# Selective scans on one core: three of eight B diagonals loaded from DRAM, softplus terms added by DMAs, the rate product made once

## The chip, the core and the metric

The kernel runs on one core of a Trainium2 chip. The metric is device time in microseconds (us) for one launch. The core has a matrix engine (PE, with its weight loads shown as PEld), a vector engine (DVE), an activation engine (ACT), a general engine (POOL), an engine that mainly issues transfers (SP), and 16 DMA engines. Each engine works through its own instructions in program order and waits on semaphores for the others.

## What is computed

Two layers run one after the other on an image of 256 x 256 tokens with 128 channels, all in float32. The first is a row-wise attention with four heads. The second, which takes most of the time, is a selective state-space layer. Its core, cut to what matters here:

```python
delta = jax.nn.softplus(dts + dt_bias[None, :, :, None])
def step(h, inp):
    d_t, x_t, B_t, C_t = inp
    dA = jnp.exp(d_t[..., None] * As)
    h = dA * h + (d_t * x_t)[..., None] * B_t[:, :, None, :]
    y = jnp.einsum('bkdn,bkn->bkd', h, C_t)
    return (h, y)
```

It runs over 65,536 tokens in four orders (along the rows, across them, and both backwards), with 256 inner channels and 16 states per channel. `dts` is itself a product of an 8-row matrix with a small weight (the "rate product").

## The kernel before

`scans` does the four orders one after the other. A `Block` is 1,024 tokens of one order; there are 64 blocks per order, 256 in all. Channels lie on partitions, in two halves of 128 (`h`), and tokens lie along the free dimension. For each block the body runs 32 steps `s`; step `s` is state `m = s // 2` and half `h = s % 2`. One step has these parts, on these engines:

- **recur** (L853): the recurrence itself is one DVE scan instruction over 1,024 tokens (L858). It reads the decay `da` (SBUF) and the input `mm` (PSUM) and writes `hs`. After the second half a small DVE reduction saves the state (L863), and POOL multiplies both halves of `hs` by C, held in `cc` (L865).
- **turn** (L841): PE writes delta * x * B, turned so that channels lie on partitions, into `mm`. There are only two `mm` buffers, used in rotation, so turn of step s+1 goes into one while the scan of step s reads the other. The 1,024 tokens are eight tiles of 128. For four of them (`DJ`) PE multiplies `dxt` by a diagonal matrix `dg` whose diagonal holds B (L846); a float32 product takes two instructions. For the other four ACT has already scaled `dxt` by B into `but`, and PE only transposes that (L848, one instruction).
- **scale** (L830): ACT makes the diagonals, `dg = identity * B` (L833), and the scaled tiles `but` (L835), three states ahead of use. Rings `dg`, `but` and `cc` have four places.
- **decay** (L837): ACT makes `da = exp(delta * A)` (L839), four steps ahead.
- **collect** (L869): PE transposes the `hs` tiles, after POOL's multiply, and adds them up in the PSUM tiles `y` (L617), three states behind. `share` sets how many a step takes.
- **fetch** (L825): SP issues the load of one row of C to all partitions, 512 KB, into `cc[m % 4]`; it waits until POOL has finished with that place.

Between those, each block prepares its successor: `begin` returns a list of pieces, each with the step at which it is issued, before or after that step's scan. `rate` (steps 6 and 8, L750) writes the rate product into an `mm` buffer, ACT takes its absolute value (L759), then exp, log, one plus and one minus (L762 to L774, 2,048 elements each). POOL adds two correction terms to the log at steps 11 to 14 (L780, L777). At steps 18 and 20 `rate` makes the same product again, and DVE forms `delta = max(product, 0) + lw` (L783). At steps 22 and 24 PE turns `delta` (`turn_rate`, L790, again in an `mm` buffer) and DVE multiplies it by x (`times_x`, L794). At steps 6 and 8 DVE adds the finished `y` to the running output (`evict`, L898). All loads of the stage are issued by SP: at step 0 `load_tokens` loads B (`bt`, 64 KB, L727) and x (`xk`, 1 MB, L728) for the next block, at step 8 the output is stored (L902), at step 16 it is loaded (L948), at step 21 come the rates (L724). The order is written out by hand in `body` (L908).

Of the kernel before, what the change touches and what calls it, by code (L numbers as in the profile page):

```python
# [29 lines left out]
AF = mybir.ActivationFunctionType  # L30
ALU = mybir.AluOpType
# [588 lines left out]
def scans(tc, io, c):  # L620
# [19 lines left out]
    with tc.tile_pool(name="e_w", bufs=1) as wp, tc.tile_pool(name="e_1", bufs=1) as sb1, tc.tile_pool(  # L640
# [11 lines left out]
        def ring(name, n, shape, pool=wp):  # L652
            return [pool.tile(shape, F32, name=f"{name}{i}") for i in range(n)]

        DJ = NJ // 2
        xks = ring("xk", 1, [P, NJ, DI])

        dts = ring("dt", 1, [P, TB])
# [26 lines left out]
        class Block:  # L685
# [39 lines left out]

            def load_tokens(self):
                nc.sync.dma_start(out=self.as_rows(self.bt), in_=self.rows(io["bk"][self.S.k]))  # L727
                nc.sync.dma_start(out=self.as_rows(self.xk), in_=self.rows(io["xk"]))  # L728

            def advance(self, now, after):  # L730
                if self.pieces is None:
# [5 lines left out]
        def begin(B):  # L737
# [19 lines left out]

            def size(h):
                nc.scalar.activation(B.e[:, h, :], B.pu[h], AF.Abs)  # L759

            def exp():
                nc.scalar.activation(B.e, B.e, AF.Exp, scale=-1.0)  # L762
# [10 lines left out]

                nc.scalar.activation(B.w, B.w, AF.Identity, scale=-1.0, bias=1.0)  # L774

            def less(h):
                nc.gpsimd.tensor_tensor(B.lw[:, h, :], B.lw[:, h, :], B.w[:, h, :], ALU.add)  # L777

            def log1p(h):
                nc.gpsimd.tensor_tensor(B.lw[:, h, :], B.lw[:, h, :], B.e[:, h, :], ALU.add)  # L780

            def softplus(h):
                nc.vector.scalar_tensor_tensor(B.delta[:, h, :], B.pu[h], 0.0, B.lw[:, h, :], ALU.max, ALU.add)  # L783

            def turn_rate(i):
                B.pt = mm().rearrange("p (j d) -> p j d", d=DI)
# [5 lines left out]
            def times_x(i):  # L792
# [12 lines left out]
                (8, True, size, 1),  # L805
                (9, True, exp),
                (10, True, log),
                (11, True, log1p, 0),
                (11, True, one_plus),
                (12, True, log1p, 1),  # L810
                (12, True, rest),
                (13, True, less, 0),
                (14, True, less, 1),

                (18, False, rate, 0),
                (18, True, softplus, 0),
                (20, False, rate, 1),
                (20, True, softplus, 1),
                (22, False, turn_rate, 0),
                (22, True, times_x, 0),  # L820
                (24, False, turn_rate, 1),
# [3 lines left out]
        def fetch(B, m):  # L825
            nc.sync.dma_start(out=ccs[m % 4], in_=B.S.C[m : m + 1, B.where()].partition_broadcast(P))

        def scale(B, m, h):  # L830
            dg, bu = dgs[m % 4], bus[m % 4]
            for j in range(h * DJ // 2, (h + 1) * DJ // 2):
                nc.scalar.activation(dg[:, j, :], c.ident, AF.Copy, scale=B.bt[:, B.slot(j), m : m + 1])  # L833
                at = B.slot(DJ + j)
                nc.scalar.activation(bu[:, j, :], B.dxt[:, DJ + j, :], AF.Copy, scale=B.bt[:, at, m : m + 1])  # L835

# [66 lines left out]

        U = NH * DS

        share = {6: 0, 7: 8, 8: 0, 18: 3, 20: 3, 22: 5, 24: 5}

        def body(blocks, before, after):  # L908

# [15 lines left out]
            if before is None:  # L925
                blocks[0].load()
                blocks[0].load_tokens()
                blocks[0].advance(U, True)
                blocks[0].free = set(range(NJ // PB))
                blocks[1].load()  # L930
                for m in range(4):
                    fetch(blocks[0], m)
                for u in range(3 * NH):
                    do(scale, u)
                for u in range(4):
                    do(decay, u)
                do(turn, 0)
            for x, B in enumerate(blocks):
                nxt = at_hand.get(x + 1)
                for s in range(U):  # L940
                    u = x * U + s
                    m, h = divmod(s, NH)
                    if s == 0 and nxt:
                        nxt.load_tokens()
                    if s == 21 and x + 2 in at_hand:
                        at_hand[x + 2].load()
                    if s == 16:
                        nc.sync.dma_start(out=B.as_rows(B.y), in_=B.rows(io["y"]))  # L948
                    if nxt:
                        nxt.advance(s, False)  # L950
                    recur(B, m, h)
                    do(turn, u + 1)
                    if at(u - LAG * NH):
                        waiting.extend((*at(u - LAG * NH), j) for j in range(NJ))
                    collect_some(len(waiting) if s == LAG * NH - 1 else share.get(s, 10))
                    if x - 1 in at_hand and s in (6, 8):
                        evict(at_hand[x - 1], B, (s - 6) // 2)
                    if nxt:
                        nxt.advance(s, True)
                    do(decay, u + 4)  # L960
                    if u == 0:
                        nc.scalar.preload_act_table_set("natural_log_exp_and_others")
                    do(scale, u + 3 * NH)
                    if h == NH - 1 and at(u + 1 + 3 * NH):
                        fetch(*at(u + 1 + 3 * NH)[:2])
            if not after:
# [8 lines left out]
        passes = (n - 2) // LOOP  # L975
        first = (n - passes * LOOP) // 4 * 2
        order = [Scan(x, k) for x, k in enumerate((0, 2, 1, 3))]
        for x, S in enumerate(order):
            starts = [Block(S, b) for b in range(first)]
            ends = [Block(S, b) for b in range(first + passes * LOOP, n)]  # L980
# [17 lines left out]
def output(tc, io, c):  # L998
# [73 lines left out]
    "dc1": (KD // 2 * RC, NT),  # L1072
    "dcT": (KD // 2 * RC, NT),
    "y": (NT, DI),
}


# [56 lines left out]
```

## Time and profile before

| | us |
|---|---|
| median of 3 runs | 28440.62 (28439.84 to 28441.89) |
| span of the profiled execution | 28447.5 |
| first to last scan instruction | 4780.7 to 27653.0 |

| stretch of 20,000 us inside the scans (6,000 to 26,000 us) | PE | DVE | ACT | POOL | DMA |
|---|---|---|---|---|---|
| busy us | 19004.87 | 18514.86 | 19439.47 | 18833.56 | 0.39 of 16 engines |

The profiled span is 7 us above the median, 0.02%. "Busy" counts the time an engine spends inside instructions; the waits view counts how long an engine was idle before an instruction and which other engine's instruction ended that; the timeline lists instructions in order of time with the idle time before each in brackets. "<-" in a group's name reads "is made from".

### The profile page before, as it was taken

To read this page: it belongs to the slowest core of one execution; us is meant where nothing else is said; L and a number is where in the kernel's file an instruction comes from. 1 tells how busy PE (TensorE), PEld (TensorE's weight loads), DVE (VectorE), ACT (ScalarE), POOL (GpSimd) and SP (SyncE) were. 2 spreads that over 40 slices of the span, in tenths; PEclk is the share of its full clock that TensorE was granted. 3 is DMA by queue.
4 is the path that set the end of the run, shared out by engine and by line. 5 is a ranking of instruction groups with operands and counts; after the bars stand their busy time and mean duration, and the time that the engine had idled before them with its cause. 6 is when DMAs were issued, how large, how long until landed. Compare 5 with 4: busy or idle time off the path is not lost. (4 is left out here: it accounts for less than half of the span.)

```text
span 28447.5 us, 528099 instructions
## 1 busy us (share of the span) xinstructions
PE 26610.1 (94%) x196490; PEld 22529.2 (79%) x196490; DVE 24922.2 (88%) x24253; ACT 25332.4 (89%) x49673; POOL 22944.4 (81%) x10118
## 2 busy tenths in 40 slices
PE   8999996999999999999999999999999999999998
PEld 3555444888888888888888888888888888888884
DVE  4777665999999999999999999999999999999987
ACT  6875224999999999999999999999999999999987
POOL 2443002999999999999999999999999999999983
PEclk9999998999999999999999999999999999999999
DMA  5112345433433333333334333333333333333335
GB/s 206 55 50 71 111 116 115 132 132 129 133 130 133 132 131 132 132 131 132 128 132 133 131 133 132 131 132 129 132 132 130 133 132 129 132 130 132 133 132 172
DMA packets 1923996, 3630.07 MB, mean 128 GB/s; under 512 B 532297, under 2 KB 1240009, under 8 KB 1889490
## 3 DMA queue, kind: packets, MB, share of 16 engines
q1 hardware_dynamic: 1424722, 3339.77, 34.6%
q10 hardware_dynamic: 496640, 255.88, 3.2%
q8 instruction: 1568, 25.69, 0.4%
q14 instruction: 1066, 8.73, 0.1%
HBM read 3002.42 MB, written 592.84 MB: 126 GB/s over the span
## 5 line engine op out<-in xcount | busy, mean ns | idle before, releaser
L865 POOL TENSOR_TENSOR hs<-hs,cc 128x1024 f32<-128x1024 f32 x8192 | 19202.5, 2380 | 1346.1 <-DVE state L863 679.9
L858 DVE TENSOR_TENSOR_SCAN hs<-da,state,mm 128x1024 f32<-128x1024 f32 x8192 | 18976.6, 2340 | 1465.4 <-PE mm L848 1074.7
L846 PE MATMUL mm<-dg,dxt 128*128 128x128 f32 x65536 | 9305.0, 287 | 1065.1 <-DVE hs L858 886.1
L846 PEld LDWEIGHTS mm<-dg,dxt 128*128 128x128 f32 x65536 | 8328.4, 199 | 2257.9 <-DVE hs L858 1897.8
L839 ACT ACTIVATE da<-delta,A 128x1024 f32<-128x1024 f32 x8192 | 9328.4, 1139 | 112.2 <-PEq L984 76.0
L617 PE MATMUL y<-ident,hs 128*128 128x128 f32 x65536 | 8511.4, 275 | 1.4 <-POOL hs L865 1.4
L835 ACT ACTIVATE but<-dxt,bt 128x256 f32<-128x256 f32 x16384 | 8150.2, 497 | 11.4 <-DVE dxt L794 11.4
L617 PEld LDWEIGHTS y<-ident,hs 128*128 128x128 f32 x65536 | 7494.1, 143 | 1.9 <-POOL hs L865 1.9
L833 ACT ACTIVATE dg<-ident,bt 128x128 f32<-128x128 f32 x16384 | 6393.1, 390 | 0.2
L848 PE MATMUL mm<-ident,but 128*128 128x128 f32 x32768 | 5092.5, 280 | 0.0
L848 PEld LDWEIGHTS mm<-ident,but 128*128 128x128 f32 x32768 | 4011.4, 146 | 0.0
L750 PE MATMUL mm<-dt,dtw 9*128 9x512 f32 x4096 | 2033.0, 615 | 265.9 <-DMA bt<-mid_bk 184.5
L385 POOL TENSOR_TENSOR an<-ex,rs 128x1024 f32<-128x1024 f32 x512 | 970.2, 1895 | 1024.5 <-PE tp L394 566.3
L780 POOL TENSOR_TENSOR lw<-lw,e 128x1024 f32<-128x1024 f32 x512 | 1207.7, 2384 | 336.3 <-ACT lw L766 336.3
L750 PEld LDWEIGHTS mm<-dt,dtw 9*128 9x128 f32 x4096 | 680.7, 184 | 959.5 <-issue 733.3
L500 POOL MEMSET pad<- 128x10 f32 x32 | 3.7, 117 | 1650.0 <-PE ps L537 1639.9
L777 POOL TENSOR_TENSOR lw<-lw,w 128x1024 f32<-128x1024 f32 x512 | 1202.9, 2375 | 0.0
L537 PE MATMUL ps<-pad,w 128*128 128x512 f32 x2048 | 954.8, 610 | 161.0 <-ACT xi L525 161.0
L372 ACT ACTIVATE ex<-sc,nm 128x256 f32<-128x256 f32 x2048 | 1013.7, 499 | 0.4
L759 ACT ACTIVATE e<-mm 128x1024 f32<-128x1024 f32 x512 | 524.7, 1025 | 522.1 <-PE mm L750 521.9
L355 DVE CUSTOM_DVE_ANT_0 sc<-ps,bias 128x256 f32<-128x256 f32 x2048 | 746.2, 421 | 117.3 <-PE ps L340 117.3
L394 PEld LDWEIGHTS tp<-ident,an 128*128 128x128 f32 x4096 | 467.5, 141 | 470.7 <-POOL an L385 235.1
(137 smaller groups left out, 18522.4 us busy)
## 6 DMA issues: line engine op xcount, KB each, us to landing
cc<-mid_dc SPq DMA_DIRECT2D x2048, 512.0 KB
cc<-mid_dcT SPq DMA_DIRECT2D x2048, 512.0 KB
xk<-mid_xk SPq DMA_DIRECT2D x256, 1024.0 KB
yb<-mid_y SPq DMA_DIRECT2D x256, 1024.0 KB
mid_y<-yb SPq DMA_DIRECT2D x256, 1024.0 KB
xt<-mid_xT SPq DMA_DIRECT2D x64, 1024.0 KB
mid_xk<-xk ACTq DMA_DIRECT2D x32, 2048.0 KB
mid_y<-y ACTq DMA_DIRECT2D x32, 2048.0 KB
```

The lines of the kernel that those rows point to most:

```text
L372: nc.scalar.activation(exs[u][:, x, :], scs[u][:, e, jt, :], AF.Exp, scale=-1.0, bias=nms[u][:, e, jt : jt + 1], accum_out=sms[u][:, x : x ...
L617: nc.tensor.matmul(out, in_, c.ident, is_transpose=True, start=start, stop=stop, skip_group_check=True)
L750: nc.tensor.matmul(pu[:, q : q + T], dtw[0 : DR + 1, k, h * P : (h + 1) * P], B.dt[0 : DR + 1, q : q + T], start=True, stop=True,)
L777: nc.gpsimd.tensor_tensor(B.lw[:, h, :], B.lw[:, h, :], B.w[:, h, :], ALU.add)
L780: nc.gpsimd.tensor_tensor(B.lw[:, h, :], B.lw[:, h, :], B.e[:, h, :], ALU.add)
L833: nc.scalar.activation(dg[:, j, :], c.ident, AF.Copy, scale=B.bt[:, B.slot(j), m : m + 1])
L835: nc.scalar.activation(bu[:, j, :], B.dxt[:, DJ + j, :], AF.Copy, scale=B.bt[:, at, m : m + 1])
L839: nc.scalar.activation(da, B.delta[:, h, :], AF.Exp, scale=A[:, B.S.k * NH + h, m : m + 1])
L846: nc.tensor.matmul(d1[:, j * P : (j + 1) * P], B.dxt[:, j, hc], dg[:, j, :], start=True, stop=True)
L848: nc.tensor.transpose(d1[:, j * P : (j + 1) * P], bu[:, j - DJ, hc], c.ident)
L858: nc.vector.tensor_tensor_scan(o, d0, d1, state[:, m, h : h + 1], ALU.mult, ALU.add)
L865: nc.gpsimd.tensor_tensor(hs[:, x, :], hs[:, x, :], ccs[m % 4], ALU.mult)
```

## The change

Three things change in `scans`.

- `DJ` is 3 instead of 4, and ACT makes no diagonals. A new DRAM buffer `dgd` holds the diagonals of two blocks (16 states x 128 x 384 each). It is zeroed once before the first scan (32 transfers from a zeroed `hs`). For each block, `spread` copies the block's B values from DRAM to the diagonal places in `dgd`, with three transfers of 128 x 16 single elements; `load_tokens` issues them between `bt` and `xk`. `diagonal` then loads one state's three diagonals (128 x 384, 192 KB) into `dg`, at the first half of each state, three states ahead.
- Right after the absolute value ACT also writes `delta = relu(product)`. POOL's four additions and DVE's two softplus instructions go; instead POOL issues three DMAs that add `lw`, `e` and `w` into `delta` in place, at steps 12, 15 and 18. Since all three write `delta`, each waits for the one before.
- `rate` is made once, at steps 6 and 8; `share` no longer has entries for steps 18 and 20.

```diff
-        DJ = NJ // 2
+        DJ = 3
...
             def load_tokens(self):
                 nc.sync.dma_start(out=self.as_rows(self.bt), in_=self.rows(io["bk"][self.S.k]))
+                self.spread()
                 nc.sync.dma_start(out=self.as_rows(self.xk), in_=self.rows(io["xk"]))
+
+            def diagonals(self):
+                return io["dgd"][self.b % 2]
+
+            def spread(self):
+                d = self.diagonals()
+                of = io["bk"][self.S.k]
+                G = N // P
+                with nc.allow_non_contiguous_dma(reason="one element of B per diagonal place"):
+                    for j in range(DJ):
+                        if self.S.across:
+                            x = of.rearrange("(g p w) c -> p g w c", p=P, w=N)
+                            x = x[:, j % G, self.where(N), :][:, j // G, :]
+                        else:
+                            x = of[self.where(), :].rearrange("(j p) c -> p j c", p=P)[:, j, :]
+                        to = bass.AP(
+                            d.tensor, d.offset + j * P, ((DJ * P + 1, P), (P * DJ * P, DS), (1, 1))
+                        )
+                        nc.sync.dma_start(out=to, in_=x.unsqueeze(2))
...
             def size(h):
                 nc.scalar.activation(B.e[:, h, :], B.pu[h], AF.Abs)
+                nc.scalar.activation(B.delta[:, h, :], B.pu[h], AF.Relu)
...
-            def less(h):
-                nc.gpsimd.tensor_tensor(B.lw[:, h, :], B.lw[:, h, :], B.w[:, h, :], ALU.add)
-
-            def log1p(h):
-                nc.gpsimd.tensor_tensor(B.lw[:, h, :], B.lw[:, h, :], B.e[:, h, :], ALU.add)
-
-            def softplus(h):
-                nc.vector.scalar_tensor_tensor(B.delta[:, h, :], B.pu[h], 0.0, B.lw[:, h, :], ALU.max, ALU.add)
+            def add(name):
+                nc.gpsimd.dma_start(out=B.delta, in_=getattr(B, name), accum_op=ALU.add)
...
                 (10, True, log),
-                (11, True, log1p, 0),
                 (11, True, one_plus),
-                (12, True, log1p, 1),
                 (12, True, rest),
-                (13, True, less, 0),
-                (14, True, less, 1),
-
-                (18, False, rate, 0),
-                (18, True, softplus, 0),
-                (20, False, rate, 1),
-                (20, True, softplus, 1),
+                (12, True, add, "lw"),
+                (15, True, add, "e"),
+                (18, True, add, "w"),
                 (22, False, turn_rate, 0),
...
+        def diagonal(B, m):
+            nc.sync.dma_start(out=dgs[m % 4].rearrange("p j q -> p (j q)"), in_=B.diagonals()[m])
...
         def scale(B, m, h):
-            dg, bu = dgs[m % 4], bus[m % 4]
-            for j in range(h * DJ // 2, (h + 1) * DJ // 2):
-                nc.scalar.activation(dg[:, j, :], c.ident, AF.Copy, scale=B.bt[:, B.slot(j), m : m + 1])
+            bu = bus[m % 4]
+            nb = NJ - DJ
+            for j in range(h * nb // 2, (h + 1) * nb // 2):
                 at = B.slot(DJ + j)
                 nc.scalar.activation(bu[:, j, :], B.dxt[:, DJ + j, :], AF.Copy, scale=B.bt[:, at, m : m + 1])
...
-        share = {6: 0, 7: 8, 8: 0, 18: 3, 20: 3, 22: 5, 24: 5}
+        share = {6: 0, 7: 8, 8: 0, 22: 5, 24: 5}
...
                     do(scale, u + 3 * NH)
+                    if h == 0 and at(u + 3 * NH):
+                        diagonal(*at(u + 3 * NH)[:2])
                     if h == NH - 1 and at(u + 1 + 3 * NH):
                         fetch(*at(u + 1 + 3 * NH)[:2])
...
+        nc.vector.memset(hss[0], 0.0)
+        for m in range(DS):
+            for x in range(2):
+                nc.sync.dma_start(
+                    out=io["dgd"][x, m], in_=hss[0].rearrange("p h t -> p (h t)")[:, 0 : DJ * P]
+                )
```

3 lines of the change are left out of this document (added).

## The prediction, made before the changed kernel was run

> **What bounds the kernel now.** I read the page first, then the busy time of the engines inside the scans, the waits there, and the timelines of one block. The scan instruction starts first at 4,780.7 us and last at 27,653 us, so the scans take 22,875 us of the 28,447.5, or 89.4 us for each of 256 blocks. Nothing outside them changes. The stretch of 20,000 us holds 7,159 scans, 223.7 blocks. The columns after the stretch are busy us (instructions) of PE, PEld, DVE, ACT and POOL, the clock, the DMA share and GB/s:
>
> ```profile
> 6000.00:26000.00 20000.00, 19004.87 (x150319) 17361.51 (x150320) 18514.86 (x12531) 19439.47 (x37147) 18833.56 (x8052) 0.97 0.39 131
> ```
>
> All four engines are over 92% busy, so the shares name no bound. The waits do (total us, times, longest):
>
> ```profile
> DVE hs L858 <- PE mm L848: 940.3, 1135, 2.1
> POOL hs L865 <- DVE state L863: 577.9, 247, 11.2
> DVE hs L858 <- ACT dg L833: 151.3, 215, 3.3
> DVE delta L783 <- PE mm L750: 76.9, 182, 0.7
> ```
>
> POOL, when idle, waits for DVE. DVE waits for PE in 1,135 places, about five per block, 4.2 us per block. The timeline of DVE shows where (start, length, what, idle before):
>
> ```profile
> 12140.06 4.58 DVE L858 TENSOR_TENSOR_SCAN hs<-da,state,mm 128x1024 f32<-128x1024 f32 x2
> ...
> 12147.30 1.22 DVE L783 SCALAR_TENSOR_TENSOR delta<-mm,lw 128x1024 f32<-128x1024 f32 x1 [0.17 <-POOL lw L777]
> 12148.89 2.35 DVE L858 TENSOR_TENSOR_SCAN hs<-da,state,mm 128x1024 f32<-128x1024 f32 x1 [0.37 <-ACT dg L833]
> ...
> 12153.62 1.20 DVE L783 SCALAR_TENSOR_TENSOR delta<-mm,lw 128x1024 f32<-128x1024 f32 x1
> 12156.28 2.35 DVE L858 TENSOR_TENSOR_SCAN hs<-da,state,mm 128x1024 f32<-128x1024 f32 x1 [1.47 <-PE mm L848]
> ```
>
> Undisturbed, two scans take 4.58 us and a state costs 4.73, with no gap: DVE sets the pace. Gaps come only where an extra product takes an `mm` buffer (steps 6, 8, 18, 20, 22, 24); then the next turn can start only when the running scan has ended. So a block is 82.8 us of DVE work (18,514.86 / 223.7) and 6.6 us of gaps. Relief of PE, ACT and POOL counts only where it shortens a gap.
>
> **What the change removes from DVE's path, per block.** Two softplus instructions at 1.22 us: 2.4. The gaps around them (0.17, 0.37 and 1.47 above; 0.39 and 1.29 a block earlier): 2.0. Waits for `dg` from ACT elsewhere: 151.3 / 223.7 = 0.7, less the 0.37 already counted, 0.3. One tile less by product: eight product instructions span 1.06 us, ten transposes 1.25, so two products for one transpose saves about 0.14 us per turn, of which the four turns that DVE still waits for (steps 6, 8, 22, 24) show 0.5. Together 5.2, and 0.3 for the 76.9 us of waits before softplus: **5.5 us**, 1,410 us over 256 blocks.
>
> What costs nothing, and why: ACT gains two relus (Abs takes 1.02 each) and 16 more scaled tiles at 0.50, but loses 64 diagonals at 0.39, 15 us net. The relu holds an `mm` buffer 0.9 us longer: in one block Abs started at 12025.49, and the turn into that buffer at 12027.17 would start 0.3 later; its scan is due at 12029.9 and the turn takes 1.5, so this stays covered; uncovered it is 0.3 to 0.9 twice. POOL loses four multiplies' worth, 9.5 us. PE loses two rate products at 1.98 and 4.5 us in turns. Zeroing `dgd` is 32 transfers at up to 0.7 us before the first scan: 20 us, bounds 0 and 30.
>
> **What it adds, first: `spread` on SP's queue.** SP issues at step 0 in this order: `cc` for state 3, `bt`, three spreads, `xk`, then `dg` for state 3, `cc` for state 4. In the block whose first scan starts at 12097.16 (t0):
>
> ```profile
> 12102.70 0.33 SPq L826 DMA_DIRECT2D cc<-mid_dc  x1
> 12103.38 0.38 SPq L727 DMA_DIRECT2D bt<-mid_bk  x1
> 12104.14 0.38 SPq L728 DMA_DIRECT2D xk<-mid_xk  x1
> ```
>
> The first of them waits for POOL to finish state 15, two multiplies after t0, and so will it in the changed kernel. What the DMA engines then carry, read in stretches of 1 us, keeps the order of issue: 750 packets under 512 B (`bt`, 1,024 packets of 64 B) in the stretch from 12105, the last 306 in the next, then the 1 KB packets of `xk`, about 360 per us, until 12109.3, t0 + 12.2. `dg` comes next: 192 KB at 350 GB/s is 0.6 us, and I allow 0.9 for its completion, as long as a `cc` takes from issue to first packet. So it is there at t0 + 13.7 + S, S being the time of the spreads. PE needs it for the turn of step 6, which must end with scan 5 at t0 + 14.05 and takes 1.4: due at t0 + 12.65. **The stall is S + 1.0**; PE stands, its transposes queue behind, and DVE with it. Nothing later in the block gives it back, since DVE sets the pace.
>
> S is 3 x 2,048 single elements. The trace has none of 4 bytes; the smallest are these 64-byte reads of B from DRAM, in 1 us:
>
> ```profile
> DMA packets 937, 0.14 MB, mean 139 GB/s; under 512 B 879, under 2 KB 929, under 8 KB 937
> ```
>
> At some 900 per us S is 6.8. From below: the convolution's 64-byte writes of B ran at 2,723 packets in 2 us, S = 4.5. From above: each element priced as a 1 KB packet, 360 per us, S = 17. I take 6.8, the same DRAM rows read: stall 7.8, bounds 5.5 and 18. On 64-byte rows neither direction shows a penalty for size. The Trainium skill ("DMA: Bandwidth & Descriptors", Specifications) says that a transfer under 512 B makes the DMA engine read, modify and write; if that doubled the write price of 4.5, S would be 9.0, and the whole change 12.0 per block, 31,540.
>
> **Second: the adding DMAs on POOL.** Queued behind each are POOL's multiplies, and PE's `turn_rate` at step 22 waits for the last. POOL's timeline, where scan 11 ended at 12041.53:
>
> ```profile
> 12041.92 4.73 POOL L865 TENSOR_TENSOR hs<-hs,cc 128x1024 f32<-128x1024 f32 x2 [0.36 <-DVE state L863]
> 12046.60 4.73 POOL L780 TENSOR_TENSOR lw<-lw,e 128x1024 f32<-128x1024 f32 x2
> ```
>
> POOL begins state 5 as soon as its scan ends, and two multiplies take 4.7. Counting from the end of scan 11, with p for POOL's issue of a DMA and D from issue to landing: state 5 is done at 5.1 and `lw` issued at 5.1 + p; states 6 and 7 follow, `e` is issued at 14.5 + 2p; after state 8 `w` must wait for `e`, so it lands at 14.5 + 3p + max(4.7, D) + D. Without softplus scan 22 ends at 26.0; `turn_rate` (1.04) must start by 25.0. **The stall is 3p + D + max(4.7, D) - 10.5.** `log` is no brake: it ended at 12041.4.
>
> p and D are not in the trace. p: an issue takes 0.38 on SP and 2.2 on ACT for the 2 MB `mid_y`; I take 1. D: the plain 1 MB `xk` has 2.9 us of packets; with 0.9 before and after, 4.7 is the lower bound. An add must fetch both operands, twice the bytes in: 5.7 + 1.8 = 7.5, which I take. Sharing the engines with C, `dg` and `yb`, now over half busy, gives 12 as upper bound. Stall: 3 + 15 - 10.5 = **7.5**, bounds 0 (0.1 by the formula) and 20. The skill (same page, "Anatomy of one DMA") gives 2.0 us + bytes / 436,000 for a DMA issued from POOL, 4.4 for 1 MB, an estimate; no run here shows one. With that the stall would be 1.6 and the whole change 3.9 per block, 29,470.
>
> **The sum.** Per block -5.5 + 7.8 + 7.5 = +9.8; times 256 is 2,510, and 20 for the zeroing: 28,447.5 + 2,530 = 30,978 for a profiled execution. The median lies 7 below the profiled span, so **30,970**.
>
> **Rivals.**
> - *Faster, the transfers stay off the path.* The DMA queue lets `dg` pass the spreads, and D is at its lower end. For it: engines only 39% busy. Against it: the packets kept their order. At 5.5 us of stalls per block the sign turns; without any the time is 28,447.5 - 1,410 + 20 = 27,060. Chance 13%, and 4% for ending within 0.2%, which is about what a measurement here can tell from no change.
> - *Only the spread costs.* D at 4.7, stall 0.7 (with 0.2 more for p): -5.5 + 7.8 + 0.7 = 3.0, 29,230. 18%.
> - *Single elements are dear.* S = 17: -5.5 + 18 + 7.5 = 20 per block, 33,590. For it: nothing so small is in the trace, and the places written are 1,540 B apart. 20%, a third of that beyond 34,500.
> - *The forecast*, the two stalls together within 5.5 us of 15.3 (29,570 to 32,390): 45%.
>
> The range 28,300 to 34,500 leaves out the 13% below and some 7% above. Faster 13%, same 4%, slower 83%.
>
> **What would show it.** In the changed profile: DVE busy near 80.4 us per block, softplus and its gaps gone; about 64 ACT diagonals per block gone; PE's product waiting once per block for a DMA into `dg`, about 8 us, at step 6; PE's `turn_rate` waiting for a DMA into `delta`, about 7 us, at step 22; POOL waiting some 3 us at the third add. If the wait at `dg` is much longer than 8, the single elements were mis-sized; if the wait at `delta` is missing, D was. If DVE shows neither, the queue's order was read wrongly.

## The result, and the profile after

The changed kernel takes **34435.51 us** (median of 4 runs, 34373.74 to 34447.72) against 28441.25: 1.210 times as long (95% interval 1.2086 to 1.2121). The forecast was 30,970. Slower was right, and both forecast waits are there; the loss of 5,994 us is more than twice the 2,530 that was forecast.

The stretch from 8,000 to 32,000 us of the changed kernel (columns as in the prediction):

```profile
8000.00:32000.00 24000.00, 18213.22 (x134498) 16799.18 (x134496) 17137.26 (x11492) 16614.52 (x25557) 16506.36 (x7448) 0.86 0.59 160
```

No engine is busy for more than 76% now, and PE's clock is 0.86 instead of 0.97. A block takes 112.62 us (8,192 scans from first to last, 32 to a block) instead of 89.36, so there are 213.1 blocks in the stretch and DVE works 80.4 us in each: just the work that was forecast. All else is waiting (total us, times, longest):

```profile
DVE hs L870 <- PE mm L860: 5074.4, 1269, 16.7
...
PE mm L858 <- DMA dg<-mid_dgd: 4403.9, 626, 16.4
...
PE mm L805 <- DMA delta<-w: 703.0, 213, 7.4
...
POOL delta L798 <- DMA delta<-e: 239.9, 30, 9.2
```

DVE waits for PE and PE for transfers, as forecast. But PE waits for `dg` 626 times, about three times per block, where one was forecast. The mean time from the start of one scan to the next, by step, shows where (worked out from the scans' start times; steps not listed differ by less than 0.25 us):

| step | 5 | 6 | 8 | 17 | 18 | 20 | 21 | 22 | block |
|---|---|---|---|---|---|---|---|---|---|
| before | 2.46 | 4.18 | 4.57 | 2.50 | 4.68 | 4.56 | 2.47 | 4.10 | 89.36 |
| after | 16.08 | 5.93 | 4.18 | 6.31 | 2.83 | 2.26 | 6.47 | 8.48 | 112.62 |
| difference | +13.6 | +1.75 | -0.4 | +3.8 | -1.85 | -2.3 | +4.0 | +4.4 | +23.3 |

So the gain is 4.5 us (steps 8, 18, 20), the wait behind the spread 15.4 (steps 5 and 6), and 12.2 come at steps 17, 21 and 22. DVE's timeline in one block:

```profile
15047.06 4.58 DVE L870 TENSOR_TENSOR_SCAN hs<-da,state,mm 128x1024 f32<-128x1024 f32 x2
...
15066.01 2.35 DVE L870 TENSOR_TENSOR_SCAN hs<-da,state,mm 128x1024 f32<-128x1024 f32 x1 [14.18 <-PE mm L860]
...
15104.77 2.35 DVE L870 TENSOR_TENSOR_SCAN hs<-da,state,mm 128x1024 f32<-128x1024 f32 x1 [3.86 <-PE mm L860]
```

What stands ahead of that first wait, in SP's timeline of the block:

```profile
15042.61 0.33 SPq L835 DMA_DIRECT2D cc<-mid_dc  x1
15043.36 0.38 SPq L727 DMA_DIRECT2D bt<-mid_bk  x1
15044.44 4.82 SPq L748 DMA_DIRECT2D mid_dgd<-mid_bk  x3
15049.64 3.45 SPq L729 DMA_DIRECT2D xk<-mid_xk  x1
15053.19 0.84 SPq L838 DMA_DIRECT2D dg<-mid_dgd  x1
```

The order is that of the prediction; the issues take 4.82 us for three spreads. And the packets, in stretches of 2 us from 15046, 15050 and 15056:

```profile
DMA packets 2307, 0.04 MB, mean 21 GB/s; under 512 B 2303, under 2 KB 2303, under 8 KB 2307
...
DMA packets 1509, 0.01 MB, mean 7 GB/s; under 512 B 1508, under 2 KB 1508, under 8 KB 1508
...
DMA packets 196, 0.20 MB, mean 100 GB/s; under 512 B 0, under 2 KB 196, under 8 KB 196
```

The first two rows are single elements for the most part, at 750 to 1,150 per us: near the forecast's 900. The third is `xk` behind them: 98 packets of 1 KB per us, where the kernel before moved 350. The adds, by the DMA issues (KB each, median us from issue to landing), and POOL's timeline of one block:

```profile
delta<-lw POOLq DMA_DIRECT2D x256, 1024.0 KB, 10.3
delta<-e POOLq DMA_DIRECT2D x256, 1024.0 KB, 13.1
delta<-w POOLq DMA_DIRECT2D x256, 1024.0 KB, 7.0
```

```profile
15091.36 0.89 POOL L798 DMA_DIRECT2D delta<-lw  x1
...
15102.10 0.88 POOL L798 DMA_DIRECT2D delta<-e  x1 [0.49 <-DMA delta<-lw]
15102.71 5.00 POOL L877 TENSOR_TENSOR hs<-hs,cc 128x1024 f32<-128x1024 f32 x2
15115.70 0.88 POOL L798 DMA_DIRECT2D delta<-w  x1 [8.00 <-ACT but L847]
```

The last wait is put down to ACT, but `e`, issued at 15102.10, is due at about 15115.2 by its median landing of 13.1 us: it is the add before that POOL waits for, and its multiplies with it.

### The profile page after: what moved, and what is told of

Read it like the earlier page. It is cut to its first block, busy times and chain, and to the rows that moved or that the text cites. A ratio compares the mean times of both kernels' runs of the same rounds, so it can differ in the third digit from the quotient of the medians.

```text
span 34444.9 us, 508691 instructions
## 1 busy us (share of the span) xinstructions
PE 26799.3 (78%) x186250; PEld 22886.7 (66%) x186250; DVE 24355.5 (71%) x23742; ACT 23070.5 (67%) x37897; POOL 21240.9 (62%) x9862
## 3 DMA queue, kind: packets, MB, share of 16 engines
q0 software_dynamic: 110592, 805.36, 11.4%
## 5 line engine op out<-in xcount | busy, mean ns | idle before, releaser
L858 PE MATMUL mm<-dg,dxt 128*128 128x128 f32 x49152 | 8163.4, 308 | 6092.9 <-DMA dg<-mid_dgd 5273.1
L858 PEld LDWEIGHTS mm<-dg,dxt 128*128 128x128 f32 x49152 | 6920.2, 213 | 7314.7 <-issue 5296.2
L847 ACT ACTIVATE but<-dxt,bt 128x256 f32<-128x256 f32 x20480 | 8991.1, 498 | 1107.7 <-PE mm L860 1075.1
L617 PEld LDWEIGHTS y<-ident,hs 128*128 128x128 f32 x65536 | 8015.0, 150 | 2.5 <-POOL hs L877 2.5
L860 PE MATMUL mm<-ident,but 128*128 128x128 f32 x40960 | 6457.6, 293 | 1.3 <-ACT but L847 1.1
L860 PEld LDWEIGHTS mm<-ident,but 128*128 128x128 f32 x40960 | 5349.0, 154 | 2.1 <-ACT but L847 2.1
L805 PE MATMUL mm<-ident,delta 128*128 128x128 f32 x4096 | 732.8, 339 | 857.8 <-DMA delta<-w 855.4
L809 DVE TENSOR_TENSOR dxt<-mm,xk 128x1024 f32<-128x1024 f32 x512 | 620.3, 1212 | 1083.2 <-PE mm L805 1031.7
L770 PE MATMUL mm<-dt,dtw 9*128 9x512 f32 x2048 | 1176.9, 699 | 204.2 <-DMA bt<-mid_bk 203.1
L805 PEld LDWEIGHTS mm<-ident,delta 128*128 128x128 f32 x4096 | 607.2, 176 | 932.5 <-issue 929.4
## 6 DMA issues: line engine op xcount, KB each, us to landing
delta<-lw POOLq DMA_DIRECT2D x256, 1024.0 KB, 10.3
delta<-e POOLq DMA_DIRECT2D x256, 1024.0 KB, 13.1
```

The costliest lines, as they stand in the source:

```text
L617: nc.tensor.matmul(out, in_, c.ident, is_transpose=True, start=start, stop=stop, skip_group_check=True)
L770: nc.tensor.matmul(pu[:, q : q + T], dtw[0 : DR + 1, k, h * P : (h + 1) * P], B.dt[0 : DR + 1, q : q + T], start=True, stop=True,)
L805: nc.tensor.transpose(B.pt[:, j, h * P : (h + 1) * P], B.delta[:, h, at : at + P], c.ident)
L858: nc.tensor.matmul(d1[:, j * P : (j + 1) * P], B.dxt[:, j, hc], dg[:, j, :], start=True, stop=True)
L860: nc.tensor.transpose(d1[:, j * P : (j + 1) * P], bu[:, j - DJ, hc], c.ident)
```

## The experiments

**The theory after the result:** the two waits that were forecast are the loss, each longer than its price: the spread with what it does to the transfer behind it, and a chain of adds that is longer than its slack. **Rivals:** the DMA engines are simply fuller (0.39 to 0.59 busy), so that each transfer is late wherever it stands; or POOL's or PE's new waits, not the transfers, cost. In what follows "us per block" is from first to last scan. The kernel before ran beside each (28,435 to 28,445). Of the times that the theory forecast, those of e3, e6 (an open range) and e12 came true; all others were too low, e19's by 38 us.

### One part alone

**e1_adds_only**: the kernel before (ACT makes four diagonals) with the adds and one rate product.

```diff
+                nc.scalar.activation(B.delta[:, h, :], B.pu[h], AF.Relu)
...
-                (11, True, log1p, 0),
...
+                (12, True, add, "lw"),
+                (15, True, add, "e"),
+                (18, True, add, "w"),
...
```

> The kernel before with relu, the three adding DMAs and the rate product made once, but with ACT's diagonals (DJ 4) and no DRAM diagonals. Theory A, the chain of the three adds is itself the cost: with some 0.9 us per issue and 8 us to landing the wait at turn_rate is 2.7 + 8 + 8 - 10.5 = 8 us, a block 92 to 93 us, 29,250 in all. Rival, the adds are slow only because the diagonal loads share the DMA engines: landing 5.5 us, wait 3 us, a block 88 to 89 us with ACT as the bound (86.9 us of work before, plus two relus), 28,200.

30,123 us (ratio 1.059, 1.056 to 1.062), 95.73 per block. Step 22 takes 13.51 instead of 4.10, +9.4, and this is the wait for the last add (landings 9.5, 11.0 and 7.5). Taking it off leaves 86.3, 3.0 below the kernel before, but ACT, which still makes its diagonals here, has 88.9 us of work per block (busy 92.9% from 8,000 to 26,000 us). So without the wait ACT would bind, at most 0.5 below the kernel before.

**e2_diagonals_only**: the changed kernel with the softplus of before.

```diff
-        share = {6: 0, 7: 8, 8: 0, 22: 5, 24: 5}
+        share = {6: 0, 7: 8, 8: 0, 18: 3, 20: 3, 22: 5, 24: 5}
...
-                (12, True, add, "lw"),
-                (15, True, add, "e"),
-                (18, True, add, "w"),
+                (11, True, log1p, 0),
...
+                (20, True, softplus, 1),
```

> The changed kernel with the softplus of before (rate twice, POOL's additions, DVE's softplus): the DRAM diagonals alone. Theory, queue order: the wait for dg at step 6 stays at 13 to 14 us per block, plus 1 to 2 us after it, so 103 to 105 us per block, 32,000 to 32,500. Rival, the adds' traffic makes the spread dear: the wait at step 6 falls under 9 us, a block under 98 us, under 30,700.

33,772 us (1.187, 1.184 to 1.191), 109.94 per block. Step 5 takes 16.11 and step 6 5.60, as in the changed kernel: the spread's wait needs no adds. But step 21 takes 9.16 (+6.7), with no add in the kernel. There PE waits for `dg`: its load stands in SP's order behind a `cc` load that waits for POOL, and POOL is late with its four additions. The forecasts had no such term.

**e3_no_spread**: the changed kernel without the spreads.

```diff
-                self.spread()
```

> The changed kernel without the spreads: dgd stays zero, so three of eight tiles of the input term are zero; every other transfer and instruction is there. Theory, the wait at step 6 is the spread and what it does to the xk load behind it: the wait falls from 13.6 to some 2.5 us, a block from 112.6 to about 100 us, 31,200. Rival, the diagonal loads or the adds load the DMA engines so much that dg is late anyway: the wait stays over 8 us, a block over 107 us, over 33,000.

31,016 us (1.090, 1.087 to 1.094), 99.25 per block. The spread is worth 13.4 us of the 23.3. `xk` now takes 3.6 us from the end of `bt` to its own end. Steps 17, 21 and 22 keep 6.44, 5.96 and 8.75: they owe nothing to the spread. Steps 5 and 6 are still 2.1 us longer than before.

### What the spread costs

**e4_spread_act_queue**: ACT issues the spreads.

```diff
-                        nc.sync.dma_start(out=to, in_=x.unsqueeze(2))
+                        nc.scalar.dma_start(out=to, in_=x.unsqueeze(2))
```

> The changed kernel with the three spreads issued by ACT, so on another DMA queue than xk and dg. Theory, queue order is what holds dg back: the wait at step 6 falls to 2 to 5 us, though ACT is held some 5 us by issuing; a block 100 to 103 us, 31,200 to 32,000. Rival, the scattered 4-byte writes slow every transfer beside them, whichever queue: the wait stays over 8 us, a block 107 to 112 us, 33,000 to 34,300.

32,505 us (1.143, 1.139 to 1.146), 105.20 per block. Steps 3, 4 and 5 take 6.74, 3.03 and 4.60: 7.2 us of waiting there instead of 13.6. `xk` takes 2.8 us after `bt`, but `bt` ends at t0 + 16.1 instead of 9.0, so the single elements delay what runs beside them on the other queue too. The same holds at step 3: there PE waits 4.1 us per block for the `dg` of state 2, which SP issues ahead of `bt`. ACT, held by the issues, costs little: DVE waits less than 0.1 us per block for `da` at step 3.

**e6_spread_dense**: the same 6,144 elements, written 8 B apart instead of 1,540 and more.

```diff
-                            d.tensor, d.offset + j * P, ((DJ * P + 1, P), (P * DJ * P, DS), (1, 1))
+                            d.tensor, d.offset + j * P * DS * 2, ((DS * 2, P), (2, DS), (1, 1))
```

> The changed kernel whose spreads write the same 6,144 single elements 8 bytes apart instead of 1,540 bytes and more apart; the diagonals in dgd are not filled, so the input term of three tiles is wrong. Theory A, the cost is the number of single elements: spread 7.8 us, xk behind it 7.4, the wait at step 6 still 12 us or more, over 33,900. Theory B, the scattered places in DRAM make the writes slow and hold up xk behind them: xk back to 3.6 us, the wait at step 6 9 us or less, under 33,300.

37,552 us (1.320, 1.317 to 1.324), 124.80 per block; step 5 takes 28.35. In the first two orders (medians over blocks 8 to 119) the last element ends at t0 + 21.2 instead of 16.8, and `xk` behind it takes 7.8 us. The mean hides two cases: step 5 takes 20.6 and 21.1 in the first two orders and 35.7 and 36.0 in the two backward ones, where the changed kernel takes 15.8 to 16.4 in all four. So near places are dearer than far ones, far more so in the backward orders, and the distance of 1,540 B was not the price.

### What the adds cost

**e7_adds_early**: the changed kernel with its adds issued sooner.

```diff
-                (12, True, add, "lw"),
-                (15, True, add, "e"),
-                (18, True, add, "w"),
+                (9, True, add, "e"),
+                (12, True, add, "lw"),
+                (15, True, add, "w"),
```

> The changed kernel with the adds issued at steps 9 (e), 12 (lw) and 15 (w) instead of 12, 15 and 18. Theory, the wait at turn_rate is the end of a chain of three adds: landing comes up to 4.7 us earlier, the 4.4 us at step 22 go, some of the 4.0 at step 21 too; 104 to 108.5 us per block, 32,300 to 33,400. Rival, the wait is set by the load on the DMA engines at that time and not by the chain: less than 1.5 us per block, over 34,000.

34,000 us (1.196, 1.192 to 1.199), 110.82 per block, only 1.8 less. Step 22 is back at 4.19: by then the last add has landed. But step 21 takes 11.27 and step 15 5.51 (+2.9), and there PE waits for `dg` (8.1 and 2.8 us per block). The wait has moved to `dg`.

**e8_dg_before_cc**: the changed kernel, each `dg` issued ahead of the `cc` load that waits for POOL.

```diff
...
-                    if h == 0 and at(u + 3 * NH):
-                        diagonal(*at(u + 3 * NH)[:2])
                     if h == NH - 1 and at(u + 1 + 3 * NH):
+                        diagonal(*at(u + 1 + 3 * NH)[:2])
                         fetch(*at(u + 1 + 3 * NH)[:2])
```

> The changed kernel with each diagonal load issued just before the C load that waits for POOL, not after it. Theory, dg is late at steps 17 and 21 because SP stands at the C load until POOL is done: both waits go (3.8 and 4.0 us), and at the block's start dg for state 3 goes ahead of the spread while dg for state 4 is due two scans later, which takes another 4 to 5 us; 99 to 102 us per block, 30,900 to 31,700. Rival, dg is late because its transfer shares the DMA engines with the adds: the waits at 17 and 21 stay, over 106 us per block, over 32,800.

32,109 us (1.129, 1.126 to 1.132), 103.58 per block. `dg` of state 3 now goes out ahead of the spread, and step 5 is at 2.46 (step 7 takes 7.34, +4.9, in its place). Steps 17 and 21 are at 2.47. But step 22 takes 17.10, +13.0. The waits of this kernel from 8,000 to 26,000 us:

```profile
PE mm L805 <- DMA delta<-w: 2239.1, 173, 16.2
...
PE mm L858 <- DMA dg<-mid_dgd: 814.7, 193, 7.9
```

13 us for `w`, once per block: what the changed kernel waits at steps 17, 21 and 22 (12.2) is one and the same chain of adds. The waits for `dg` at 17 and 21 only take a part of it sooner.

**e12_copies**: e1 with plain copies of `lw` (twice) and `e` in the place of the three adds.

```diff
-                nc.gpsimd.dma_start(out=B.delta, in_=getattr(B, name), accum_op=ALU.add)
+                nc.gpsimd.dma_start(out=B.delta, in_=getattr(B, name))
...
-                (18, True, add, "w"),
+                (18, True, add, "lw"),
```

> The adds-only kernel with plain copies of the same size on the same queue in place of the three adds (lw, e, lw into delta); softplus is then only lw. Theory, the add itself is dear because the DMA fetches both operands (8 KB packets took 628 ns against 311 for plain ones): landing falls from 9.5, 11.0 and 7.5 us to 5 to 7, the wait at step 22 from 9.4 to 2 to 5 us, a block from 95.7 to 88.5 to 91.5, 28,250 to 29,000. Rival, landing is set by the issue, the completion and the other queue: it stays over 8.5 us for the first two, a block over 93.5, over 29,500.

28,647 us (1.007, 1.005 to 1.009), 90.11 per block; step 22 takes 7.51 (+3.4 instead of +9.4). The landings are 7.0 to 7.6, and the queue's row (packets, MB, share of 16 engines) of e1, then of e12:

```profile
q0 software_dynamic: 110592, 805.36, 13.0%
```

```profile
q0 software_dynamic: 110592, 805.36, 6.7%
```

ACT is busy 98.3% of the time in e12 (17,697.60 of 18,000 us) and binds now. The same bytes hold the DMA engines twice as long when they add: 6.0 of the 9.4 us are the price of adding, the rest that of three transfers in series.

### Is that all, and what is the gain worth?

**e9_all_three**: the changed kernel with the adds of e7, the order of e8, and the three spreads at steps 3, 9 and 11, behind `xk`.

```diff
...
+                    if nxt and s in (3, 9, 11):
+                        nxt.spread((3, 9, 11).index(s))
...
```

> The changed kernel with all of it: adds three steps earlier, diagonal loads ahead of the C loads, and the three spreads apart, at steps 3, 9 and 11. Theory, all waits come from the order on SP's and POOL's queues: with each third of the spread under the 3 to 7 us of lead that dg has, a block comes to 83.9 us plus 2 to 5, 27,600 to 28,350, faster than before. Rival, the load on the DMA engines itself costs: over 91 us per block, slower than before.

29,995 us (1.055, 1.051 to 1.058), 95.43 per block. No spread waits any more: step 5 takes 2.47. Step 22 still takes 11.26 (+7.2), and landings are 10.0 (`e`), 11.0 (`lw`) and 12.6 (`w`). So the wait of e7 at step 21 was for the most part the chain of adds too: with `dg` out of its way it stands at step 22 again.

**e10_dve_add_dj5, e11_dve_add_dj4, e13_diag_mended_dve_add**: no adds by DMA. POOL's additions stay as before, the relu is in `delta`, and DVE adds `lw` at steps 18 and 20. ACT makes five diagonals (e10) or four (e11); e13 has the spread and the `dg` order of e9.

```diff
-                nc.vector.scalar_tensor_tensor(B.delta[:, h, :], B.pu[h], 0.0, B.lw[:, h, :], ALU.max, ALU.add)
+                nc.vector.tensor_tensor(B.delta[:, h, :], B.delta[:, h, :], B.lw[:, h, :], ALU.add)
```

> The kernel before with the rate product made once, relu on ACT, delta + lw added by DVE from SBUF at steps 18 and 20, ACT's diagonals for five tiles instead of four, no DRAM diagonals and no adding DMAs. Theory, DVE sets the pace and only the gaps that the second rate product made go: 89.4 less 2.0 of gaps and less some waits for ACT, 87 to 88 us per block, 27,850 to 28,100, 1.2 to 2% faster. Rival, ACT (86.9 us of work before, plus 1.9 for relu, less 1.8 for the fifth diagonal tile) or PE is the bound in its place: 89 us or more, no faster.

> The same with four diagonal tiles, as before. If ACT's work comes last (86.9 + 1.9 = 88.8 us) it stands at 88.5 to 89.5 us per block, 28,200 to 28,450; if DVE's pace does, it is with the five-tile version, 87 to 88.

> DRAM diagonals with their loads ahead of the C loads and the spreads in thirds at steps 3, 9 and 11, as in the run with all three; softplus by POOL's additions as before and one DVE add per half from SBUF, rate made once; no adding DMAs. Theory, with the adds gone nothing is late and DVE sets the pace: 82.8 us of work and 3.5 to 5 of gaps, 86 to 88 us per block, 27,600 to 28,100, faster than before. Rival, the transfers of the diagonals still collide (POOL's lag behind its four additions holds up SP): over 89.4, no faster.

29,514 (1.038, 1.036 to 1.039), 29,515 (1.038, 1.036 to 1.040) and 29,303 us (1.030, 1.029 to 1.032): all three missed. The group of the addition in e10, from 8,000 to 26,000 us (busy us, mean ns | idle before):

```profile
L784 DVE TENSOR_TENSOR delta<-delta,lw 128x1024 f32<-128x1024 f32 x386 | 1326.0, 3435 | 0.0
```

and that of softplus in the kernel before, from 6,000 to 26,000 us:

```profile
L783 DVE SCALAR_TENSOR_TENSOR delta<-mm,lw 128x1024 f32<-128x1024 f32 x446 | 543.7, 1219 | 82.5 <-PE mm L750 76.9 <-POOL lw L777 4.3
```

The addition has the size of the old softplus, which took 1.22 us, and takes 3.44 by mean. It waits for nothing before it; the time is inside the instruction. 510 of the 512 ran for at least nine tenths of their time beside POOL instructions; the one that ran while POOL was idle took 1.21 us. The old softplus ran beside POOL as well (511 of 512) and took 1.20 to 1.23: it had one operand in PSUM, the new addition has both in SBUF. The Trainium skill ("SBUF — State Buffer", SBUF: two separate sides) says that a DVE instruction with two SBUF inputs and a POOL instruction that reads SBUF lock the same ports, one blocking the other to its end. Most of the numbers agree: a POOL multiply takes 2.4 us, so one such wait gives at most about 3.6, and 478 of the 512 took 1.4 to 3.4. But 32 took 11.4 to 12.0, longer than one POOL instruction can explain, and no run here shows why.

**e14_later_turn**: e9, with `turn_rate` and `times_x` two steps later.

```diff
-                (22, False, turn_rate, 0),
+                (24, False, turn_rate, 0),
...
-                (24, False, turn_rate, 1),
+                (26, False, turn_rate, 1),
```

> The version with the spread in thirds, dg ahead of cc and the adds at steps 9, 12 and 15 still had 7.2 us of waiting per block at step 22 (95.4 us per block). Here turn_rate and times_x move from steps 22 and 24 to 24 and 26, and nothing else changes. If the length of the chain of adds is the cause, the wait shrinks by the two steps, 4.7 us, to about 2.5: 90.7 us per block, about 28,800 us. If the adds cost by occupying the DMA engines (dg and cc come late), the wait goes elsewhere and the time stays above 29,600.

29,500 us (1.037, 1.036 to 1.039), 93.37 per block. The wait for `w` is gone from its step, but step 23 takes 7.39 (+4.9), waiting for `dg`: of the 4.7 us of two steps of slack only 2.1 came off the block. The forecast for the rival was the nearer one.

**e15_one_add** and **e16_two_adds**: e14, with POOL making all four additions again and one DMA adding the sum, or POOL making two and DMAs adding `w` and the sum.

```diff
-                (9, True, add, "e"),
-                (12, True, add, "lw"),
-                (15, True, add, "w"),
+                (11, True, log1p, 0),
+                (12, True, log1p, 1),
+                (13, True, less, 0),
+                (14, True, less, 1),
+                (16, True, add_lw),
```

> As the kernel before it in this call (spread in thirds, dg ahead of cc, turn_rate at 24 and 26), but POOL makes its four additions as the kernel before the change did, and one DMA at step 16 adds the sum to delta in place of softplus. The chain theory: it is issued when POOL is through, near scan 17, lands 8 to 10 us later near scan 21, and no product waits for it; without waits a block is 80.4 us of DVE and about 4.5 of gaps at steps 6, 8, 24 and 26, some 86 us with POOL's 84 us of work nearly hidden: 27,600 us (27,400 to 28,000), below the kernel before. The rival: the spread and the 192 KB dg loads by themselves cost more than their issue, or POOL at 84 us holds the cc loads; then 28,500 or more.

> As the one with one add, but POOL only makes the sum of log and e (two instructions at steps 11 and 12), and two DMAs add w (step 13) and the sum (step 16) to delta. POOL has 4.7 us less to do than with one add, the chain is one landing longer (7 to 13 us). By the chain theory it is there near scan 24, just in time: 86 to 88 us per block, 27,600 to 28,200 us. If it waits at step 24 the chain is longer than I count; by the rival, that the adds' bytes cost by themselves, it is slower than the kernel with one add by more than 1 us per block.

e15: 30,013 us (1.056, 1.054 to 1.058), 95.32 per block; e16: 28,467 us (1.001, 1.000 to 1.002), 89.32; both missed. In e15 step 23 alone takes 13.32. SP's timeline ahead of such a wait:

```profile
16198.60 0.32 SPq L846 DMA_DIRECT2D dg<-mid_dgd  x1
16207.15 0.34 SPq L843 DMA_DIRECT2D cc<-mid_dc  x1
16207.84 0.39 SPq L974 DMA_DIRECT2D yb<-mid_y  x1
16208.34 0.87 SPq L846 DMA_DIRECT2D dg<-mid_dgd  x1
```

Each `dg` goes ahead of its own `cc` but behind the one of the state before. SP waits 8 us for POOL, which is behind by its additions; then the 1 MB of `yb` and, on POOL's queue at 16207.05, the add go out with `dg`, and PE gets it only at 16220. It is the coupling of e2 again, a `dg` behind a `cc` that waits for POOL. The adds' bytes alone are not the cause: of e14, e15 and e16, e15 has the fewest and waits longest. The next runs test the coupling with the same bytes.

**e17_two_adds_cc_later, e18_one_add_cc_later**: each `cc` load one state later, so that it needs POOL two states back, not one.

```diff
...
-                        fetch(*at(u + 1 + 3 * NH)[:2])
+                    if h == NH - 1 and at(u + 1 + 2 * NH):
+                        fetch(*at(u + 1 + 2 * NH)[:2])
```

> The kernel with two adds, its cc loads issued one state later, so that a cc load doesn't wait for POOL until POOL is two states behind instead of one. By the coupling theory the 3.7 us per block at step 21 go, and with them the smaller waits at 22 and 24 (0.6 and 0.7) shrink: 89.3 becomes about 85.5 us per block, 27,500 us (27,300 to 27,900), below the kernel before. By the rival, that the adds' bytes hold up dg wherever it is issued, the wait stays at 21 or moves to another step, and the time stays above 28,200.

> The kernel with one add, its cc loads one state later in the same way. POOL is two states behind after its four additions, 9.4 us, just what the later cc allows. By the coupling theory the 10.9 us per block at step 23 go: 95.3 becomes 84.5 to 87 us (POOL alone has 85 us of work), 27,300 to 28,000. By the rival it stays above 29,000.

28,460 us (1.0005, 0.9996 to 1.0014) and 28,531 us (1.003, 1.002 to 1.004). e18's block falls from 95.32 to 89.57, and step 23 from 13.32 to 3.13; but step 24 takes 8.75 (+4.7); the wait there, from 8,000 to 26,000 us:

```profile
PE mm L810 <- DMA delta<-lw: 775.9, 200, 5.0
```

The coupling is gone, with the same bytes moved, and the add itself is late: it stood behind two of POOL's multiplies. e17 doesn't gain: step 21 is back at 2.47 and step 23 takes 6.60. There POOL waits 1,025.6 us in the same stretch for `w` to land before it issues the second add, and PE's transposes into `y` wait for POOL (3.5 us per block at step 23). Both missed.

**e19_one_add_sooner**: e18, its add issued ahead of those two multiplies.

```diff
-                (16, True, add_lw),
+                (14, True, add_lw),
```

> The kernel with one add and later cc loads, its add issued at step 14, right behind POOL's fourth addition, in place of step 16: two multiplies (4.7 us) earlier. By the chain theory the 4.7 us at step 24 go: 89.6 becomes 84.5 to 86 us per block, since POOL has 85 us of work, 27,200 to 27,700 us, the first version below the kernel before. By the rival, that the add's bytes or POOL's two states of delay cost wherever it stands, the wait comes back at another step and the time stays at 28,200 or more.

**27,738 us (0.9753, 0.9739 to 0.9766)**, 86.49 per block: 2.5% below the kernel before, 38 us above the range expected. Landing is 7.8 us and no product waits for it. The stretch from 8,000 to 26,000 us:

```profile
8000.00:26000.00 18000.00, 16559.42 (x131389) 15129.23 (x131388) 16686.01 (x11231) 15974.19 (x24964) 17622.75 (x7694) 0.97 0.64 184
```

POOL is busy 97.9% and is the bound now; 1.8 us per block are left at step 21, where PE's transposes into `y` wait for POOL. The DMA engines are busier than in the changed kernel (0.64 against 0.59), and the kernel is faster than the one before. So fuller DMA engines are not by themselves the loss; what counts is what waits for a transfer. The other rival holds in part: in e2 and e15 it is POOL's lateness that holds SP and so `dg`.

The diagonals in DRAM are part of this gain, though hardly any step shows it: with ACT's diagonals and the relu ACT alone has 88.9 us of work per block (e1), more than the 86.49 of e19, where it has 76.8 (15,974.19 of 18,000 us). How the 2.5% divide among the parts of the change is not shown; no run has one add with ACT's diagonals.

## Why the prediction was right in sign and short in size

The two stalls have the causes that were forecast; two terms of the sum were too small, the transfer of `xk` behind the spread and the landing D of an add. They make most of the 13.5 us per block between the 9.8 forecast and the 23.3 measured: the stall for `dg` is 7.6 short, that for the adds 4.7, and the gain is 1.0 less. The result lies 64 us below the top of the stated range; the range reaches that far because of S = 17, which is not there, so that is luck.

- **The bound, and the gain (5.5 us per block; measured 4.5).** DVE's pace and its 80.4 us per block are as forecast. The gain is 1.0 short, in the gaps: step 8 gave 0.4, and steps 18 and 20 4.15 of the 4.4 counted for the two softplus and the gaps around them.
- **The stall for `dg` (7.8; measured 15.4): this is the step that failed.** The mechanism was right: one queue, order of issue kept, PE at step 6. The sizes, as medians over blocks 8 to 119 (in the first two orders) and counted from t0:

| | forecast | measured |
|---|---|---|
| `bt` ends | 9.3 | 9.0 |
| spreads, S | 6.8 | 7.8 |
| `xk` behind them | 2.9 | 7.4 |
| `dg` and the turn until scan 6 | 0.6 + 0.9 + 1.4 | 4.0 |
| scan 6 starts | 21.9 | 28.2 |

S was good to 1 us. The term that fell is the 2.9 of `xk`, carried over from one block of the kernel before as if a transfer's time didn't depend on what went ahead of it; the runs showed 7.4 behind the spread and 3.6 without it (e3; about the same, by median, in the kernel before). The prediction's own sign, that a wait much longer than 8 means mis-sized single elements, would have pointed at S. The last row's rest of 1.1 is mostly PE: the turn takes 2.8 instead of the 1.4 forecast, at a clock that after such a wait is at half, below. The table ends where scan 6 starts, 14.1 us late; the rest of the 15.4 is step 6 itself, which takes 1.75 longer (by means over all blocks 13.6 at step 5 and 1.75 at step 6).
- **The stall for the adds (7.5; measured 12.2).** The formula was right and D was not: 7.5 was taken for each, and 10.3, 13.1 and 7.0 were measured from the start of the issue, so that POOL's 0.88 for an issue (p, taken as 1) is inside. Since `lw` lands later than the two states' multiplies end, the chain is 5.1 + 10.3 + 13.1 + 7.0 = 35.5 against 25.0, a stall of 10.5. In e8, where nothing else waits before step 22, `turn_rate` starts 36.8 us after the end of scan 11 by median, 11.8 late; the rest of its 13.0 lies in the turns behind it, where PE's clock is 0.54 instead of 1.00. e12 shows the cause of most: adding holds the DMA engines twice as long. The forecast doubled only the bytes fetched, and took 12 as upper bound. Nor was the price for a plain transfer of 1 MB that the prediction quotes, 4.4 us, met: e12's plain copies landed in 7.0 to 7.6.
- **Its place.** Forecast at step 22 alone. That `dg` stands behind a `cc` load that waits for POOL was seen at step 0 and not asked for the other states. In the changed kernel this only splits the stall (e8), and in e7 too it mostly does (e9); but in e2, e15 and e16 it is a wait of its own.
- **The rivals.** "Only the spread costs" fell with e1. "Single elements are dear" gave 33,590, nearest to the time, but for a reason that isn't there: S is 7.8, not 17. "Transfers off the path" was wrong for this kernel; its price of no stall, 27,060, was not reached by e19 (27,738), where POOL makes its additions again and binds.
- **The sum.** -4.5 + 15.4 + 12.2 = 23.1 of the 23.3 us per block; 23.3 times 256 is 5,960 of the 5,994.

Three things stay open. Why `xk` reads slowly behind single elements: half of its packets took 46 ns, as in the kernel before, but some took far longer (mean 76 ns instead of 50 over blocks 8 to 119; the longest in the block shown 1,478), and the engines were 0.62 to 0.92 busy from 15,055 to 15,060; no run tells what the long ones waited for. Why near places are so much dearer in the backward orders (e6). And why `e` lands later than `lw` and `w`: it shares the engines with the load of `yb`, but no run took that away.

## What to carry to other kernels

Price a transfer by what goes ahead of it and by all that is issued behind it, not by its own row from another place; and for each instruction that a queue holds up, follow the queue once per turn of the loop, not only where the change stands. A chain of transfers that each wait for the last costs its length less the slack. Shortening it (three adds to one) paid only when no load stood behind a waiting one any more and the add was issued in time (e15 30,013, e18 28,531, e19 27,738), so expect each wait that is taken away to show the next. When a change loses on waits alone, a gain may still be there: here a version with one adding DMA in place of three (POOL making its additions as before), its transfers issued in time and no load behind a waiting one, is 2.5% faster instead of 21% slower.

## What the runs showed of the hardware

- **An adding DMA costs the DMA engines twice a plain one**: 13.0% of 30,094 us (e1) against 6.7% of 28,648 (e12) for the same 805 MB, 634.6 ns for an 8 KB packet in the changed kernel against 313 for a plain one in e12; 1 MB lands in 7.0 to 13.1 us (changed kernel) against 7.0 to 7.6 (e12).
- **Single elements to DRAM**: 6,144 take 7.8 us with places 1,540 B and more apart, some 4 us longer with places 8 B apart in the first two orders (in the backward ones the wait at step 5 grows by some 20 us), and the 1 MB read behind them takes 7.4 to 7.8 us instead of 3.6. In the block shown each such packet is recorded with 7 to 9 ns and the engines are 0.14 to 0.43 busy from 15,047 to 15,054, so most of the engines' time goes by between them; no run tells what sets the rate.
- **A DVE addition with both operands in SBUF** takes 3.4 us by mean beside POOL's instructions, up to 12.0, and 1.2 in the one case alone; with one operand in PSUM 1.2 beside POOL too.
- **PE's clock after a wait.** In e15 it is granted 1.00 in the four us from 16,196 and 0.50 in those from 16,220, just after a wait of 8.7 us (0.81 in the four after those). The six products of a turn took 0.83 us before the wait and 1.62 behind it:

```profile
16208.11 0.83 PE L866 MATMUL mm<-dg,dxt 128*128 128x128 f32 x6
...
16220.13 1.62 PE L866 MATMUL mm<-dg,dxt 128*128 128x128 f32 x6 [8.72 <-DMA dg<-mid_dgd]
```

The Trainium skill ("TensorE: Matmul & The Clock Gate", Part 1: The HAM clock gate) says that an idle window of about 3.4 us halves PE's clock, and that as much sustained work gives it back; these rows agree with the half, and no run here measures the window. So a wait of PE costs more than its length: the turn that ends it is slow, as step 6 of the changed kernel shows (5.93 us, of which 1.75 are new).
